# Layer 0 of a four-layer image kernel: PSUM tiles of one bank for the softmax sum and the floor, the reciprocals as side steps, the scan's total as two tiles, and a second side step on the matrix engine late in the layer

## The chip, the cores and the metric

The kernel runs on one core of a Trainium2 chip. A core has five engines with a queue each: PE (matrix multiplication; the loading of its weights is shown apart as PEld), DVE (vector), ACT (activation functions), POOL (a second vector engine) and SP, which here only starts transfers. Each engine runs its instructions in program order; semaphores make one engine wait for another. PE writes its results to PSUM, which this kernel uses as eight banks of 512 float32 values (`NB`) for each of 128 partitions; DVE and ACT read them there. All else lies in SBUF, where POOL works too, and transfers (DMA) bring data from the device's memory and back.

The metric is the device time of one execution in microseconds. Before the change it is 10293.78 us, the median of three runs (10289.03 to 10293.99).

## The reference

Input is x, four images of 128 channels and 64 x 64 pixels, in float32. Four layers follow each other. The change touches layer 0 and, in one instruction, layer 1:

```python
# layer 0, for each image; n = 4096 pixels, C = 128
x1 = conv1x1(x, v_w, v_b); x2 = conv1x1(x, q_w, q_b)
weight = conv1x1(leaky(conv1x1(x2, lw1_w, lw1_b)), lw2_w, lw2_b)
bias   = conv1x1(leaky(conv1x1(x2, bw1_w, bw1_b)), bw2_w, bw2_b)
norm = sqrt(sum(q * q, axis=0));  k = q / clip(norm, 1e-4)
logits = einsum('cn,cm->nm', k, q)
mean = logits.mean(axis=0)
sparse = relu(logits - mean * w + b);  mask = sparse != 0
attn = softmax(logits * sparse, axis=0)
attn = clip(attn * mask, 1e-08)
out = einsum('cn,nm->cm', v, attn)
y = leaky(conv3x3(out, lin_w) + lin_b) + x
```

Layer 1 is a state space scan over the 4096 pixels of each image (64 states for each of 128 channels) between a convolution and two projections, layer 2 an attention whose logits are an outer product, and layer 3 a scan over all images forward and backward, with a group normalisation behind it.

## The kernel before

**Order of the layers.** `layers01` (L1189) goes through the four images. For each it runs 128 turns of layer 0 (`turn_of`, L741), and then the scan of layer 1 (`scan_stream.tile`, L923), in whose first 16 tiles some late turns of layer 0 still run (the tail). Layer 2 of an image runs beside layers 0 and 1 of the next one: `row_weights` (L1711) in the turns of layer 0, `attend` (L1776) in the scan. Layer 3 comes at the end, after 5540 us. All instructions of these layers go through a helper that keeps them in the order of the program text, so they all have line L112 in the profile and are told apart by the names of their tiles.

**A turn.** Layer 0 treats 256 query pixels at a time, a chunk. The 4096 key pixels of a chunk are taken in 8 turns of 512, so there are 16 chunks and 128 turns; `m`, the turn's number modulo 8, is its position in the chunk. A turn works on 4 key blocks of 128 by 256 queries as one tile of 128 x 1024. Turn i issues, in this order:

| step (function, line) | engine | what it does | in the profile |
|---|---|---|---|
| image (L684) | DVE, ACT | only where a chunk has been finished (`ended`): scales it into a padded image | ypad<-acc,rows |
| weights(i) (L596) | DVE | relu(logits - cut) times logits | e<-t,lg |
| floor_of (L675) | PE | once a chunk (position 2): the floor, 1e-8 times the softmax sum, spread over the partitions | zs_rz<-rows,floor_c |
| product(i - 11) (L632) | PE | attention times values, summed over the 8 turns of a chunk | acc<-t,vT |
| logits(i + 2) (L584) | PE | keys times queries; two buffers of two banks, so those of turn i must have been read by weights(i) | lg<-rows,k |
| above(i + 1) (L591) | DVE | logits minus cut | t<-lg,rows |
| floored(i - 10) (L629) | DVE | maximum with the floor | t<-t,zs_rz |
| side steps that are not PE's, up to two | ACT, DVE, POOL | see below | |
| signs, shifted, exp | ACT, POOL, ACT | mask; subtract a bound; exponential | t<-t; e<-e,rows; e<-e |
| row weights (`beside`) | ACT | from turn 22, images 2 to 4 only | junk<-gp,... |
| masked(i - 1) (L623) | DVE or POOL | mask times exponential; on DVE in odd turns, on POOL in even ones | t<-t,e |
| sums (L608) | PE | every second turn: softmax sums Z over keys | zs_rz<-e,ones |
| one side step | PE, or another | see below | |

In a turn with `ended` the logits come before the product, because the product needs the accumulator that the image has just read.

**PSUM.** Of the eight banks, four hold the two buffers of logits (or of scan input), one ("a", `misc`) is shared by all side steps, one ("b", `other`) holds the accumulator, and two ("cd") are one tile: in layer 0 zs_rz, with Z in its first bank (`bank["zs"]`) and the reciprocals (`bank["rz"]`) and the floor (`bank["fl"]`) in the two halves of its second; in the scan `total`, over which the scan's outputs are summed. Only the last chunk's floor lies in bank "b", since "cd" is the scan's by then.

**Scale.** After a chunk's last turn its sums are turned into a scale in five steps (`scales`, L644): kept copies Z to SBUF (ACT, rows<-zs_rz, at the end of position 0), turned makes a column of it (PE, zs_rz<-quarter,rows, position 1), inverted takes the reciprocal (DVE, rzt<-zs_rz, position 2), spread brings it back over the partitions (PE, zs_rz<-ident,rzt, position 2), copied puts it into SBUF (ACT, rows<-zs_rz, position 3). They stand at fixed places in `turn_of` (`run[0][1]` to `run[0][4]`).

**Side steps.** Work that isn't bound to a turn lies in a queue of runs (`Queue`, L31), each a list of steps that is finished before the next is begun. In each turn up to two steps that are not PE's are taken after floored, and at the end either one step of PE's, if one is next, or one other. A step of PE's writes the one bank "a", and the steps behind it read it. The runs are: thresholds (L542), eight steps a chunk (two of PE's: th_ps<-rows,w_T with kbar_rep, and th_ps<-rows,lw_rep with bw_rep; then ACT's hidden and mean, DVE's times, cut, top and top_b); the 3 x 3 convolution (L696), four steps a chunk (two of PE's, then ACT and POOL, a load and a store); values in image 1; the previous scan's last outputs at the start of images 2 to 4 (`finish` and `pass_a`); and from turn 58 on the input of the next scan (`tokens_of`), one run every third turn, which has to be done by turn 120. PE never takes more than one side step in a turn.

Of the kernel before, what the change touches and what calls it, by code (L numbers as in the profile page):

```python
# [8 lines left out]
F32 = mybir.dt.float32  # L9
BF16 = mybir.dt.bfloat16  # L10
AF = mybir.ActivationFunctionType
ALU = mybir.AluOpType
# [4 lines left out]
P = 128  # L17
# [4 lines left out]
NB = 512  # L22
# [91 lines left out]
        return call  # L114


class Memory:


# [29 lines left out]
    def other(self, name, rows=P):  # L149
        return self.psb.tile([rows, NB], F32, name=name, tag="b")  # L150

    def total(self, name="total"):
        return self.pst.tile([P, self.net.T], F32, name=name, tag="cd")


class Pools:
# [14 lines left out]
    def pair(self, name):  # L171
        return self.psd.tile([P, self.T], F32, name=name, tag=name)

    def total(self, name="total"):
        return self.pst.tile([P, self.T], F32, name=name, tag=name)


class Net:
# [221 lines left out]
    def layer0(self, b, mem):  # L400
# [8 lines left out]
        S = NC * U  # L409
        LAG = U + 2  # L410
        KB = self.T // P
        Z = Block()
        Z.S, Z.LAG = S, LAG
        misc = mem.misc
# [193 lines left out]
        def sums(i):  # L608

            m = i % U  # L610
            if "zs" not in bank:
                both_banks = mem.total("zs_rz")
                bank["zs"], bank["rz"] = both_banks[:, 0:Q], both_banks[:, NB : NB + Q]
                bank["fl"] = both_banks[:, NB + Q :]
            for j in range(J):
                r = j * P // J
                pe.matmul(
                    bank["zs"][r : r + P // J, :], self.ones[:, 0 : P // J], e[i][:, j, :],
                    start=(m == 0), stop=(m == U - 1),
                )  # L620
            mem.give(e.pop(i))
# [21 lines left out]

        def scales(c):  # L644

            zt, rz = {}, {}

            def kept():
                zt[0] = zcopy[c] = row("z")
                act.copy(zt[0], bank["zs"])  # L650

            def turned():
                for i in range(Q // P):
                    pe.matmul(
                        bank["rz"][:, i : i + 1], zt[0][:, bass.ts(i, P)], self.quarter, start=True, stop=True,
                    )

            def inverted():
                rz[0] = mem.fixed("rzt", [P, Q // P])
                dve.reciprocal(rz[0], bank["rz"][:, 0 : Q // P])  # L660

            def spread():
                for i in range(Q // P):
                    pe.matmul(
                        bank["rz"][:, bass.ts(i, P)], rz[0][:, i : i + 1].to_broadcast([P, P]), self.ident,
                        start=True, stop=True,
                    )

            def copied():
                scale[c] = row("scale")  # L670
                act.copy(scale[c], bank["rz"])

            return kept, turned, inverted, spread, copied

        def floor_of(c):  # L675

            if c == NC - 1:
                bank["fl"] = bank["b"][:, Q:]
            pe.matmul(bank["fl"], self.floor_c, zcopy.pop(c), start=True, stop=True)

        def square(x):
            return x.rearrange("p (a b) -> p a b", b=IMG)
# [48 lines left out]

        due = {}
        beside = self.row_weights(b - 1, mem) if b else lambda i: None
        run = {}

        def others(left):
            while queue and not queue.on_pe() and left:
                queue.step()
                left -= 1

        def turn_of(i):  # L741
            c, m = divmod(i, U)
            w = i - LAG
            ended = i in due
            scaled = U < i <= S + 3
            if i == 4:
                begin()
            if ended:
                d = due.pop(i)
                image(d)  # L750
                if d:
                    queue.add(convolved(d - 1))
                if d == NC - 1:
                    queue.add(convolved(d))
            if i < S:
                weights(i)
            if ended:
                logits(i + 2)
            fresh = 0 <= w < S and w % U == 0
            if fresh and w < S - U:  # L760
                floor_of(w // U)
            if 0 <= w - 1 < S:
                product(w - 1)
                if (w - 1) % U == U - 1:
                    due[i + 1] = (w - 1) // U
            if fresh and w == S - U:
                floor_of(w // U)
            if not ended:
                logits(i + 2)
            above(i + 1)  # L770
            if 0 <= w < S:
                floored(w)
            if scaled and m == 2:
                run[0][2]()
            if scaled and m == 3:
                run[0][4]()
            others(2)
            if i and i <= S and (i - 1) % 2:
                signs(i - 1)
            if i < S:  # L780
                shifted(i)
            beside(i)
            if 0 < i <= S:
                masked(i - 1)
            if scaled and m == 1:
                run[0][1]()
            if scaled and m == 2:
                run[0][3]()
            if 0 < i <= S and i % 2 == 0:
                sums(i - 2)  # L790
                sums(i - 1)
            if i and i <= S and i % U == 0:
                run[0] = scales(i // U - 1)
                run[0][0]()
            if i < S and m == 0 and c + 1 < NC:
                given(c + 1)
            if m == 1 and i < S and c + 1 < NC:
                queue.first(thresholds(c + 1))
            if i == S - 1:
                mem.give(*k.values())  # L800
            if queue and queue.on_pe():
                queue.step()
            elif queue:
                others(1)
# [22 lines left out]
    def scan_stream(self, mem, blocks, side, early=lambda k, n: None):  # L827
# [65 lines left out]
        def begun(B):  # L893
            if B.first:
                B.totals[0] = mem.total()
                for j in range(W // NB):
                    s = bass.ts(j, NB)
                    pe.matmul(B.totals[0][:, s], B.diag_d, B.u[:, s], start=True, stop=False)
                if B.begun:
                    B.begun()  # L900

        def summed(i):

            k, n = items[i]
            B = blocks[k]
            for j in range(W // NB):
                s = bass.ts(j, NB)
                for m in range(i, i + Q):
                    g = of(m)[1]
                    r = (g // O) * S  # L910
                    pe.matmul(
                        B.totals[0][r : r + S, s], self.gather[:, g % O, :], p[m][:, s],
                        start=False, stop=(B.last and n == G - Q),
                    )
            for m in range(i, i + Q):
                mem.give(p.pop(m))
# [337 lines left out]
    def layer1(self, b, mem, before, after):  # L1254
# [38 lines left out]
        def prepared(w):  # L1293

            B = Block()
            B.b_rows, B.c_rows = self.bc1[w % 2, 0], self.bc1[w % 2, 1]
            B.rows = self.d1[w % 2]

            def begin():
                B.u = mem.take("u")  # L1300
                for g in groups:
                    g.u = B.u
                if w:
                    fetch(w)

            def shared():
                for g in groups:
                    g.parts = B.parts

            def done(total):  # L1310
                dve.tensor_tensor(xc[w], xc[w], total, ALU.add)
                kept["queue"].first(*finish(w))

            groups, totals = [], {}
            for i in range(SG):
                g = Block()
                g.first, g.last, g.totals, g.done = i == 0, i == SG - 1, totals, done
                g.decay, g.carry, g.diag_d = self.A1[i], carry[:, i, :], self.diagD1
                g.way, g.at = slice(None), W - 1
                g.rows = B.rows  # L1320
                g.begun = lambda: mem.give(B.u)

                def reps(g=g, i=i):
                    n = slice(i * G, (i + 1) * G)
                    if i == 0:
                        shared()
                    g.b_rep, g.c_rep = (self.rep_rows(mem.take("rep"), sp, r[n, :]) for r in (B.b_rows, B.c_rows))

                def over(g=g, i=i):
                    mem.give(g.b_rep, g.c_rep)  # L1330
                    if i == SG - 1:
                        mem.give(*B.held)

                g.reps, g.over = reps, over
                groups.append(g)
            return B, groups, begin
# [604 lines left out]
    def layer3(self):  # L1941
# [4 lines left out]
        with self.pool("l3w", 1) as big, self.pool("l3", 2) as work, self.pool("l3t", 2) as tmp, \  # L1946
# [263 lines left out]
            for forward in (True, False):  # L2210
                for ch in range(NT) if forward else reversed(range(NT)):
# [3 lines left out]
                    for j in range(J):  # L2215
# [19 lines left out]
                        B.reps = reps  # L2235

                        def done(total, K=K, j=j):
                            dve.tensor_tensor(K.sz[:, j, :], K.sz[:, j, :], total, ALU.mult)
                            if j == J - 1:
                                into(K.number + 1, post(K))  # L2240

# [131 lines left out]
```

## Time and profile before

| | us |
|---|---|
| median of 3 runs | 10293.78 |
| the profiled execution, time | 10278.34 |
| its span | 10276.6 |
| PE busy | 8433.4 (82%) |
| DVE busy | 9216.1 (90%) |
| ACT busy | 6242.1 (61%) |
| POOL busy | 8158.9 (79%) |
| layer 0 of image 1, 84 to 725: PE / DVE busy of 641 | 623.8 / 604.2 |
| layer 0 of image 2, 1615 to 2330: PE / DVE busy of 715 | 673.5 / 627.8 |
| layer 0 of image 3, 3220 to 3930: PE / DVE busy of 710 | 667.6 / 627.4 |
| layer 0 of image 4, 4815 to 5525: PE / DVE busy of 710 | 667.8 / 626.1 |
| layer 3, 5540 to 10276: PE / DVE busy of 4736 | 3637.6 / 4172.2 |

A line of the timeline has the start, the length, the engine, the source line, the operation, the tile that is written, an arrow, the tiles that are read, shapes and the number of instructions put together; in square brackets stands the idle time before it and what ended it. A line of the waits has the waiting engine and tile, the engine and tile it waited for, and then the sum in microseconds, the number of waits and the longest. A matrix product in float32 is two passes, so four products show as "x8". The profile names as releaser the event that came last.

### The profile page before, as it was taken

What the parts mean: (1) busy time and instruction counts of PE and PEld (TensorE: products, weight loads), DVE (VectorE), ACT (ScalarE), POOL (GpSimd) and SP (SyncE); (2) the same over time, 40 slices, a digit from 0 to 9 for tenths busy, and PEclk for the clock granted to TensorE, in tenths of its full rate; (3) what the DMA queues carried; (4) which work ended last, traced back from release to release, by engine and by line L of the source; (5) the groups of instructions that cost most, each with busy time, mean ns of one, the idle gap of its engine ahead of it and who ended that gap; (6) DMA issues with size and microseconds to landing.
All of it is one profiled execution on the core that took longest, in us unless ns stands there. A gap on an engine that the chain in (4) does not pass through costs nothing. (4 is left out here: it accounts for less than half of the span.)

```text
span 10276.6 us, 105974 instructions
## 1 busy us (share of the span) xinstructions
PE 8433.4 (82%) x35245; PEld 4118.2 (40%) x35320; DVE 9216.1 (90%) x6491; ACT 6242.1 (61%) x9105; POOL 8158.9 (79%) x3574
## 2 busy tenths in 40 slices
PE   8996778998888998888998877877777777777774
PEld 6772225773334774333774322322222222222221
DVE  7999999889999889999889998079999999999996
ACT  3335554666774666765565765466666666667664
POOL 5778887778887778887767887079999999999986
PEclk9998778999999999998999988989898899998886
DMA  1027882018884017885006986078788888888886
GB/s 40 17 65 193 205 198 59 18 48 200 212 209 109 18 29 182 210 209 145 24 18 146 212 201 154 16 179 208 197 205 201 203 206 205 221 223 222 225 225 176
DMA packets 523460, 1549.32 MB, mean 151 GB/s; under 512 B 85760, under 2 KB 126336, under 8 KB 522912
## 3 DMA queue, kind: packets, MB, share of 16 engines
q1 hardware_dynamic: 522912, 1542.54, 60.7%
q8 instruction: 280, 4.59, 0.2%
q14 instruction: 268, 2.20, 0.1%
HBM read 1346.52 MB, written 132.83 MB: 144 GB/s over the span
## 5 line engine op out<-in xcount | busy, mean ns | idle before, releaser
L112 DVE TENSOR_TENSOR_SCAN h<-da,carry,db 128x1024 f32<-128x1024 f32 x1536 | 3603.5, 2346 | 151.2 <-DVE db L112 2.4
L112 POOL TENSOR_TENSOR p<-h,rep 128x1024 f32<-128x1024 f32 x1024 | 2403.6, 2356 | 588.0 <-DVE h L112 523.1
L112 POOL TENSOR_TENSOR p<-h,c_rep 128x1024 f32<-128x1024 f32 x1024 | 2405.5, 2361 | 301.9 <-DVE h L112 282.9
L112 PE MATMUL db<-parts,sel 96*128 96x512 bf16 x4096 | 1366.5, 419 | 1330.1 <-DVE h L112 1322.5
L112 ACT ACTIVATE da<-row,A 128x1024 f32<-128x1024 f32 x1536 | 1760.2, 1147 | 184.6 <-DMA row<-d 182.8
L112 POOL TENSOR_TENSOR e<-e,rows 128x1024 f32<-128x1024 f32 x512 | 1261.1, 2468 | 458.2 <-DVE e L112 345.1
L112 PEld LDWEIGHTS <-sel 96*128 96x128 bf16 x4096 | 313.6, 101 | 2764.5 <-DVE h L112 1605.3
L112 DVE TENSOR_TENSOR_SCAN h<-db,carry,x 128x1024 f32<-128x1024 f32 x512 | 1195.5, 2335 | 132.0 <-ACT db L112 96.0
L112 ACT ACTIVATE db<-db,A 128x1024 f32<-128x1024 f32 x512 | 555.1, 1084 | 1034.4 <-PE db L112 985.8
L112 PE MATMUL total<-p,gather 128*32 128x512 f32 x8192 | 1171.6, 691 | 8.7 <-POOL p L112 8.7
L112 ACT ACTIVATE e<-e 128x1024 f32<-128x1024 f32 x512 | 540.6, 1056 | 933.6 <-POOL e L112 933.4
L112 PE MATMUL lg<-rows,k 128*128 128x256 f32 x4096 | 989.3, 385 | 56.1 <-DVE e L112 35.6
L112 PE MATMUL acc<-t,vT 128*128 128x256 f32 x4096 | 1002.7, 390 | 13.2 <-DVE t L112 7.6
L112 DVE TENSOR_TENSOR db<-b_rep,db 128x1024 f32<-128x1024 f32 x768 | 927.3, 1207 | 56.6 <-PE db L112 56.6
L112 PE MATMUL acc<-e,values 128*128 128x512 f32 x1536 | 852.5, 649 | 129.9 <-ACT e L112 107.2
L112 DVE TENSOR_TENSOR db<-rep,db 128x1024 f32<-128x1024 f32 x768 | 928.0, 1208 | 32.4 <-PE db L112 32.1
L112 PEld LDWEIGHTS acc<-t,vT 128*128 128x128 f32 x4096 | 783.5, 194 | 193.5 <-issue 59.5
L112 PEld LDWEIGHTS lg<-rows,k 128*128 128x128 f32 x4096 | 777.3, 192 | 204.1 <-issue 80.8
L112 ACT ACT_TABLE_LOAD x609 | 781.3, 1283 | 38.6 <-DMA r<-y 12.0
L112 DVE TENSOR_TENSOR t<-lg,rows 128x1024 f32<-128x1024 f32 x512 | 622.9, 1217 | 123.9 <-PE lg L112 123.2
L112 DVE TENSOR_TENSOR t<-t,zs_rz 128x1024 f32<-128x1024 f32 x480 | 580.5, 1209 | 134.2 <-ACT rows L112 127.4
L112 ACT ACTIVATE e<-gq,below,fcol 128x512 f32<-128x512 f32 x768 | 611.1, 805 | 141.6 <-PE acc L112 141.5
(241 smaller groups left out, 12353.0 us busy)
## 6 DMA issues: line engine op xcount, KB each, us to landing
row<-d SPq DMA_DIRECT2D x2048, 512.0 KB
rep<-bc SPq DMA_DIRECT2D x128, 512.0 KB
parts<-split SPq DMA_DIRECT2D x960, 64.0 KB
d<-delta SPq DMA_DIRECT2D x80, 384.0 KB
r<-y SPq DMA_DIRECT2D x48, 512.0 KB
res<-x SPq DMA_DIRECT2D x32, 512.0 KB
b_rep<-bc SPq DMA_DIRECT2D x32, 512.0 KB
c_rep<-bc SPq DMA_DIRECT2D x32, 512.0 KB
```

The costliest lines, as they stand in the source:

```text
L112: return self.tc.keep_in_program_order(method(*args, **kwargs))
```

## The change

`Memory.total` no longer gives one tile of two banks but a small object `Total` with two tiles of one bank, "c" and "d"; `Pools.total`, which layer 3 uses, still gives one tile, as two halves and as a whole. In layer 0 Z takes a tile in "c" and the floor one in "d". The reciprocals take a tile in the side steps' bank "a", and four of the five scale steps become a run in the queue, put in at position 1 (the thresholds, put in after it, go ahead of it); kept stays where it was. From turn 58 (`FIRST`) on, a turn whose queue is longer than 8 steps takes a further step of PE's in the middle of the turn, if one is next, and up to two more other steps near its end, before the last one. In layer 1 the sum of the scan's total into xc is two instructions of 512 columns instead of one of 1024.

```diff
+class Total:
+    def __init__(self, parts, whole=None):
+        self.parts, self.whole = parts, whole
...
-    def total(self, name="total"):
-        return self.pst.tile([P, self.net.T], F32, name=name, tag="cd")
+    def bank(self, tag, name):
+        return self.pst.tile([P, NB], F32, name=name, tag=tag)
+
+    def total(self):
+        return Total([self.bank(tag, "total") for tag in "cd"])
...
-    def total(self, name="total"):
-        return self.pst.tile([P, self.T], F32, name=name, tag=name)
+    def total(self):
+        t = self.pst.tile([P, self.T], F32, name="total", tag="total")
+        return Total([t[:, bass.ts(j, NB)] for j in range(self.T // NB)], t)
...
             if "zs" not in bank:
-                both_banks = mem.total("zs_rz")
-                bank["zs"], bank["rz"] = both_banks[:, 0:Q], both_banks[:, NB : NB + Q]
-                bank["fl"] = both_banks[:, NB + Q :]
+                bank["zs"] = mem.bank("c", "zs")[:, 0:Q]
...
             def turned():
+                held["rz"] = misc("rz_ps")
                 for i in range(Q // P):
                     pe.matmul(
-                        bank["rz"][:, i : i + 1], zt[0][:, bass.ts(i, P)], self.quarter, start=True, stop=True,
+                        held["rz"][:, i : i + 1], zcopy[c][:, bass.ts(i, P)], self.quarter, start=True, stop=True,
                     )
...
             def spread():
+                held["rz"] = misc("rz_ps")
...
             def copied():
                 scale[c] = row("scale")
-                act.copy(scale[c], bank["rz"])
-
-            return kept, turned, inverted, spread, copied
+                act.copy(scale[c], held["rz"][:, 0:Q])
+
+            return [on_pe(turned), inverted, on_pe(spread), copied]
+
+        def kept(c):
+            zcopy[c] = row("z")
+            act.copy(zcopy[c], bank["zs"])
...
             if c == NC - 1:
                 bank["fl"] = bank["b"][:, Q:]
-            pe.matmul(bank["fl"], self.floor_c, zcopy.pop(c), start=True, stop=True)
+            elif "fl" not in bank:
+                bank["fl"] = mem.bank("d", "fl")[:, 0:Q]
+            pe.matmul(bank["fl"], self.floor_c, zcopy[c], start=True, stop=True)
...
             if 0 <= w < S:
                 floored(w)
-            if scaled and m == 2:
-                run[0][2]()
-            if scaled and m == 3:
-                run[0][4]()
             others(2)
+            much = i >= FIRST and len(queue) > 8
+            if much and queue.on_pe():
+                queue.step()
...
             if 0 < i <= S:
                 masked(i - 1)
-            if scaled and m == 1:
-                run[0][1]()
-            if scaled and m == 2:
-                run[0][3]()
...
             if i and i <= S and i % U == 0:
-                run[0] = scales(i // U - 1)
-                run[0][0]()
+                kept(i // U - 1)
...
+            if m == 1 and U < i <= S + 1:
+                queue.first(scales(c - 1))
             if m == 1 and i < S and c + 1 < NC:
                 queue.first(thresholds(c + 1))
...
+            if much:
+                others(2)
             if queue and queue.on_pe():
                 queue.step()
             elif queue:
                 others(1)
...
             def done(total):
-                dve.tensor_tensor(xc[w], xc[w], total, ALU.add)
+                for c in range(C):
+                    t = xc[w][:, bass.ts(c, NB)]
+                    dve.tensor_tensor(t, t, total.parts[c], ALU.add)
                 kept["queue"].first(*finish(w))
```

## The prediction

> **What bounds the kernel now.** First the busy time in stretches of 50 us through layer 0 of the second image (columns: stretch, length, then PE, PEld, DVE, ACT, POOL busy with their instructions, clock, DMA share, GB/s).
>
> ```profile
> 1800.00:1850.00 50.00, 48.56 (x280) 38.47 (x279) 44.00 (x42) 31.48 (x46) 37.20 (x16) 1.00 0.04 11
> 2050.00:2100.00 50.00, 50.00 (x264) 37.73 (x265) 43.69 (x43) 35.45 (x55) 36.34 (x16) 1.00 0.12 35
> 2100.00:2150.00 50.00, 47.10 (x272) 36.91 (x271) 44.25 (x39) 33.50 (x48) 36.18 (x16) 1.00 0.06 17
> ```
>
> PE is busy 47 to 50 of 50 us, DVE 44. PE sets the pace here, so an edit is worth the PE idle time that it removes or makes. Next the waits, of PE between 1690 and 2260 us (nearly the whole of that image's layer 0), and of DVE in all of it.
>
> ```profile
> PE zs_rz L112 <- DVE t L112: 14.5, 15, 2.3
> PE lg L112 <- DVE e L112: 3.8, 4, 1.8
> DVE t L112 <- ACT rows L112: 41.6, 13, 3.7
> DVE t L112 <- PE lg L112: 31.8, 31, 2.1
> ```
>
> PE's largest wait is for DVE's floored, before a write into zs_rz; DVE's is for an ACT copy. The timelines show both in one place.
>
> ```profile
> 1826.10 1.89 PE L112 MATMUL lg<-rows,k 128*128 128x256 f32 x8
> 1829.43 0.60 PE L112 MATMUL zs_rz<-quarter,rows 128*128 128x1 f32 x4 [1.44 <-DVE t L112]
> 1827.77 0.35 ACT L112 COPY rows<-zs_rz 128x256 f32<-128x256 f32 x1
> 1828.15 1.22 DVE L112 TENSOR_TENSOR t<-t,zs_rz 128x1024 f32<-128x1024 f32 x1 [3.55 <-ACT rows L112]
> ```
>
> The copy kept, late behind the row weights on ACT, holds floored; floored holds PE's turned, which writes the bank that it reads. PE is idle for 1.44 us, once in a chunk of eight turns.
>
> By the Trainium skill (PSUM — Partial Sum Buffer, section "PSUM bank collisions raise a hardware error") engines collide only within a bank; different banks run side by side. Kept reads one bank and floored the other, yet floored waits 3.55 us: the tile they share orders them, not the chip. By that rule alone this wait would cost nothing today; by the row it does.
>
> Last, turn 66. Turned runs at position 1 of a chunk; the last in this image's 128 turns stands at 2257.12 (turn 121), and counting back by eight puts 1956.54 in turn 65.
>
> ```profile
> 1960.34 1.89 PE L112 MATMUL lg<-rows,k 128*128 128x256 f32 x8
> 1962.07 0.61 PE L112 MATMUL zs_rz<-ident,rzt 128*128 128x128 f32 x4
> 1962.61 1.07 PE L112 MATMUL zs_rz<-e,ones 128*32 128x256 f32 x16
> 1963.61 0.70 PE L112 MATMUL th_ps<-rows,lw_rep 64*128 64x256 f32 x2
> 1964.14 0.59 PE L112 MATMUL th_ps<-rows,bw_rep 64*128 64x256 f32 x2
> 1964.66 1.99 PE L112 MATMUL lg<-rows,k 128*128 128x256 f32 x8
> 1959.80 1.21 DVE L112 TENSOR_TENSOR t<-t,zs_rz 128x1024 f32<-128x1024 f32 x1
> 1961.01 0.41 DVE L112 TENSOR_TENSOR ypad<-acc,rows 128x256 f32<-128x256 f32 x1
> 1961.33 1.21 DVE L112 SCALAR_TENSOR_TENSOR e<-t,lg 128x1024 f32<-128x1024 f32 x1
> 1964.88 0.48 DVE L112 SCALAR_TENSOR_TENSOR rows<-th_ps,lw_b,rows 128x256 f32<-128x256 f32 x1
> 1965.40 0.48 DVE L112 SCALAR_TENSOR_TENSOR rows<-th_ps,bw_b,rows 128x256 f32<-128x256 f32 x1
> 1966.93 0.42 DVE L112 TENSOR_TENSOR rows<-rows,rows 128x256 f32<-128x256 f32 x1
> ```
>
> What to see: weights(67) ends at 1962.54, and the logits that need its buffer start at 1964.66. DVE is 2.1 us ahead, no more.
>
> **The change, part by part.**
>
> *Tiles of their own.* Turned no longer waits for floored, nor do the sums. At most 14.5 us of PE idle time goes in images 2 to 4. I take 13, since some of it only brings PE sooner to a wait for weights (3.8 us today). In image 1, whose ACT has no row weights, the same waits are five of 0.3 us: 1.5. The 4.97 us before the sums at 2293.59 go too, but there DVE runs without a gap from 2281.67 to 2306.95 and is the bound: 0, at best 5 an image. Sum: 3 x 13 + 1.5 = **40.5 us gained**, bounds 30 to 65.
>
> *Reciprocals as side steps.* Per chunk two small matmul groups (0.54 us each from start to start), a reciprocal (0.16) and a copy (0.35) move from turns 1 to 3 of a chunk to turns 4 to 6, behind the thresholds; they issue no DMA. The scale is needed ten turns after it is queued, so nothing is late. The convolution's taps slip two turns, and with them POOL's add, SP's load of the residual and store of x1. The store that the next scan's first load needs comes at turn 56, the load at 60, some 21 us later: cover enough; without it that load would be late by what is missing. At the start of images 2 to 4 the previous scan's last output steps, pass_a's matmuls and SP's stores of g2, h2 and x2 among them, end at turn 23, not 16; row weights first read at 19, after the last step that feeds them (18). All steps share the one bank "a", where today PE waits for a reader once between 1690 and 2260 (h_ps, 0.7 us). I take 0; if PE met a late copy before the taps as it now meets floored, 1.44 us a chunk.
>
> *Second PE step.* Walking the queue by the source, 17 turns per image get it: 58, 59, 66, 67, 68, 74, 75, 82, 83, 85, 90, 91, 98, 106, 107, 114, 115. What costs is that the readers follow in the same turn.
>
> (a) In 58, 66, 90, 98, 106 and 114 the second threshold matmuls run in mid turn, and times, cut and top come right after on DVE. In turn 66's rows: they start where the spread stands, 1962.07, and end 1.12 later (1963.61 to 1964.73 today), 1963.19. DVE, free at 1960.93, waits till 1963.27, and behind it wait image, weights, POOL's shifted and PE's logits. Times 0.52, cut 0.40, top 0.34, image 0.32, weights 1.21: done at 1966.06. PE ends the sums at 1964.1 (1963.13 + 1.0) and, in this turn, takes the logits before the product because an image has just ended: it waits **2.0 us**. Six times: 12.
>
> (b) In 59, 67, 91, 107 and 115 turned, reciprocal and spread fall in one turn: PE waits for drain 0.06, hand-over 0.11, reciprocal 0.16, hand-over 0.07 = 0.4, five times: 2.
>
> (c) In 74, 82 and 90 the second threshold matmuls meet ACT's hidden behind exp, row weights (1.22 each) or a softplus with two table loads (1.28 + 0.69 + 1.28). In turn 82 the logits end at 2047.72; first threshold matmuls 1.11 and sums 1.0 make PE ready at 2049.8, while the row weights hold ACT till 2050.5 and hidden (0.47) ends at 2050.97: 1.2. For the two longer ones 2.4: 6 in all, bounds 0 and 12. Image 1: 0.5.
>
> (d) In 68 DVE's reciprocal waits for ACT's root with two table loads; in 85 the taps wait for a copy behind exp: 1.25 each, bounds 0 and 3. Image 1: 1.
>
> Images 2 to 4: 12 + 2 + 6 + 2.5 = 22.5; image 1: 12 + 2 + 1.5 = 15.5. **Lost: 83 us**, bounds 30 (half of (a), little else) and 125.
>
> PE's granted clock matters too: after 3.67 us of idling the logits at 1638.22 took 3.75 us, not 1.9; after 1.82 us at 2110.17 they took 1.97. The new gaps are like the second, so the sum has nothing for it. The Trainium skill (TensorE: Matmul & The Clock Gate, section "What's actually happening") halves the clock after an idle window of about 3.4 us; by it the sum stays as it is, while the 2.86 us after a 2.76 us gap at 1657.15 speak for 0.9 more on the longest.
>
> *Total as two tiles.* 16 sums over 1024 columns (1.14 from start to start) become two of 512 (0.59, as the residual's at 1648.70): 0.04 x 16, about 1 us. Layer 3 keeps its one tile: 0.
>
> **Sum.** -40.5 + 83 + 1 = +43.5 us on the profiled 10278.3, so 10321.8. The median of the runs is 15.4 above the profiled one; on that basis 10337.
>
> **Rivals.** *A, faster.* DVE loses 41.6 us of waits an image; should that lead stay, the stalls of (a) vanish. It decides once weights ends within 1.0 us of the second threshold matmuls. Against it: in (a) DVE waits for a matmul that PE reaches after its own logits, so lead doesn't help. Cost zero: 10293.8 - 40.5 + 1 = 10254; with the tails 10234. Chance 0.20. *B, no difference:* half of the stalls hidden, 10293.8 - 40.5 + 41.5 + 1 = 10296. Chance 0.12. *C, slower still:* the gap moves instead of going, with bank "a" holding PE before the taps in each chunk; the 40.5 are not gained: 10378. For it: one bank for four kinds of steps. Against: that single 0.7 us today. Chance 0.13. *That it doesn't do what it says:* floored and sums wait as before through another tile; for the stalls that is C's time and sits in its chance. My forecast: 0.55, its own range 10316 to 10365.
>
> **Numbers.** A change within 0.2% (20.6 us) can't be told from none. Faster is A, 0.20; the same is B, 0.12; slower is the forecast and C, 0.68. The range runs from 10255, where only A's better half is left out, to 10395, C with a little of the clock's loss.
>
> **What would show it.** Right: no wait of floored for an ACT copy; no gap before the turned matmuls; six gaps of about 2 us per image before logits, each after times, cut and top with DVE waiting for th_ps; PE at 50 of 50 before turn 58; each image's first 58 turns shorter, the rest longer. Wrong: if logits follow the sums in those turns without a gap, A holds; if PE waits before conv_ps all through, C.

## The result, and the profile after

The changed kernel takes 10393.9 us (median of 4 runs, 10387.7 to 10402.6) against 10293.9 (4 runs, 10289.0 to 10297.5) for the kernel before on the same chip: ratio 1.0098, 95% interval 1.0081 to 1.0116. It is 100 us slower; 43.5 were forecast. The profiled execution took 10394.0 us (span 10392.2), that of before 10278.3 (span 10276.6). That pair is 115.6 us apart, because the one of before lay 15 us under its median.

Set side by side by the starts of DVE's weights (512 in each kernel) and of its scans (2048), in us:

| stretch, summed over the images | before | after | difference |
|---|---|---|---|
| layer 0, turn 0 to turn 56 | 1128.6 | 1117.2 | -11.4 |
| layer 0, turn 56 to the first scan tile | 1536.8 | 1638.4 | +101.6 |
| layer 1's scans of images 1 to 3 | 2768.4 | 2790.8 | +22.4 |
| first scan tile of image 4 to the last scan instruction | 4708.8 | 4711.0 | +2.2 |

The first part got shorter and the part with the second PE step longer, as the forecast has it. Busy times in stretches of 50 us of the changed kernel's second image (columns as before: stretch, length, PE, PEld, DVE, ACT, POOL, clock, DMA share, GB/s); turn 58 lies at about 1935:

```profile
1830.00:1880.00 50.00, 49.50 (x281) 38.50 (x281) 47.57 (x42) 32.24 (x48) 36.98 (x16) 1.00 0.05 12
...
2130.00:2180.00 50.00, 46.62 (x247) 36.76 (x245) 42.54 (x40) 31.78 (x45) 32.91 (x15) 0.93 0.04 12
```

Before turn 58 PE is busy for 49.5 of 50 us and the idle time that the turned matmuls had is gone. Later PE loses 3.4 us in 50, and the clock is 0.93, not 1.00. The waits of PE and DVE between 1718 and 2306 us (us in total, times, longest):

```profile
DVE t L112 <- PE lg L112: 35.1, 30, 3.5
DVE rows L112 <- PE th_ps L112: 27.2, 8, 5.9
PE lg L112 <- DVE e L112: 22.2, 14, 3.1
PE th_ps L112 <- ACT rows L112: 6.6, 4, 2.6
```

PE's 14.5 us before zs_rz and DVE's 41.6 us for the ACT copy are gone. In their place DVE waits 27.2 us for the threshold matmuls, and PE 22.2 us (3.8 before) for DVE's weights. The timeline shows one such place, turn 98 of image 2:

```profile
2167.34 1.89 PE L112 MATMUL lg<-rows,k 128*128 128x256 f32 x8
2169.20 0.70 PE L112 MATMUL th_ps<-rows,lw_rep 64*128 64x256 f32 x2
2169.74 0.59 PE L112 MATMUL th_ps<-rows,bw_rep 64*128 64x256 f32 x2
2170.19 2.37 POOL L112 TENSOR_TENSOR t<-t,e 128x1024 f32<-128x1024 f32 x1 [1.64 <-ACT t L112]
2170.26 1.07 PE L112 MATMUL zs<-e,ones 128*32 128x256 f32 x16
2170.45 0.48 DVE L112 SCALAR_TENSOR_TENSOR rows<-th_ps,lw_b,rows 128x256 f32<-128x256 f32 x1 [3.06 <-PE th_ps L112]
2170.97 0.49 DVE L112 SCALAR_TENSOR_TENSOR rows<-th_ps,bw_b,rows 128x256 f32<-128x256 f32 x1
2171.49 1.35 DVE L112 TENSOR_TENSOR rows<-rows,rows 128x256 f32<-128x256 f32 x1
2172.76 0.41 DVE L112 TENSOR_TENSOR ypad<-acc,rows 128x256 f32<-128x256 f32 x1
2173.10 1.20 DVE L112 SCALAR_TENSOR_TENSOR e<-t,lg 128x1024 f32<-128x1024 f32 x1
...
2174.45 3.58 PE L112 MATMUL lg<-rows,k 128*128 128x256 f32 x8 [3.12 <-DVE e L112]
```

DVE is 3.06 us early and waits for matmuls that PE reaches only after its logits. Times, cut, top, image and weights follow, and PE, done with the sums at 2171.3, waits 3.12 us. Two things are new: top takes 1.35 us, not the 0.42 of turn 66 before, and the logits behind the gap take 3.58 us, not 1.9, at a granted clock of 0.54. Such gaps stand before the logits after turns 58, 66, 90, 98, 106 and 114 of every image, 13.3 us together in image 1 and 16.6 to 17.0 in the others, 64 in all. After turn 24, 19 logits of the four images took over 3 us, 3.55 on average: 18 of the 24 behind these gaps, and those of turn 75 in image 2 (3.78 us), shortly behind another wait of PE, of 2.57 us for an ACT copy before the threshold matmuls.

### The profile page after: what moved, and what is told of

The parts are those of the page before. It is cut to its first block, busy times and chain, and to the rows that moved or that the text cites. A ratio compares the mean times of both kernels' runs of the same rounds, so it can differ in the third digit from the quotient of the medians.

```text
span 10392.2 us, 105806 instructions
## 1 busy us (share of the span) xinstructions
PE 8492.4 (82%) x35320; PEld 4128.5 (40%) x35320; DVE 9232.9 (89%) x6507; ACT 6240.6 (60%) x9105; POOL 8168.8 (79%) x3574
## 3 DMA queue, kind: packets, MB, share of 16 engines
q14 instruction: 268, 2.19, 0.1%
## 5 line engine op out<-in xcount | busy, mean ns | idle before, releaser
L112 PE MATMUL lg<-rows,k 128*128 128x256 f32 x4096 | 1021.5, 394 | 129.4 <-DVE e L112 107.0
L112 DVE TENSOR_TENSOR db<-rep,db 128x1024 f32<-128x1024 f32 x768 | 928.2, 1209 | 40.7 <-PE db L112 40.5
L112 POOL TENSOR_TENSOR t<-t,e 128x1024 f32<-128x1024 f32 x256 | 616.0, 2406 | 119.4 <-ACT t L112 119.4
```

Of the source, the lines that this page charges most:

```text
L112: return self.tc.keep_in_program_order(method(*args, **kwargs))
```

## The experiments

Theory M: the tiles of their own gain what was forecast, and the second threshold matmuls in mid turn, with their readers behind them, lose it again and more. Rivals: the scan total as two tiles costs the scans (S); the wait moves to another place of the chunk, bank "a" above all (C). All kernels were timed in five rounds against the kernel before on their chip.

| kernel | median us | before | ratio, 95% interval |
|---|---|---|---|
| own_banks | 10253.8 | 10297.5 | 0.9960, 0.9946 to 0.9973 |
| own_again (the same kernel) | 10266.4 | 10293.8 | 0.9972, 0.9961 to 0.9984 |
| side_early | 10270.3 | 10288.5 | 0.9983, 0.9974 to 0.9992 |
| hold_second | 10291.1 | 10297.5 | 0.9995, 0.9987 to 1.0004 |
| hold_both | 10294.1 | 10293.8 | 0.9999, 0.9990 to 1.0008 |
| six | 10295.7 | 10288.5 | 1.0009, 1.0000 to 1.0018 |
| top_later | 10342.7 | 10288.5 | 1.0051, 1.0037 to 1.0065 |
| warm4 | 10366.4 | 10288.5 | 1.0075, 1.0062 to 1.0088 |
| warm | 10372.7 | 10297.5 | 1.0073, 1.0061 to 1.0086 |
| one_tile | 10404.7 | 10297.5 | 1.0107, 1.0093 to 1.0121 |

A second measure is layer 0 alone in the profiled executions (the first two rows of the table above, added): before 2665.4, after 2755.6, own_banks 2618.1, own_again 2625.0, side_early 2628.9, six 2660.8, hold_both 2665.6, hold_second 2676.3, top_later 2708.0, warm4 2727.9, warm 2737.9, one_tile 2776.7. It leaves out the scans, whose time differs from one profiled execution to the next (see the end).

**own_banks: the tiles alone.** The kernel before, with

```diff
-                both_banks = mem.total("zs_rz")
-                bank["zs"], bank["rz"] = both_banks[:, 0:Q], both_banks[:, NB : NB + Q]
-                bank["fl"] = both_banks[:, NB + Q :]
+                both = mem.bank("c", "zs_rz")
+                bank["zs"], bank["rz"] = both[:, 0:Q], both[:, Q:]
+                bank["fl"] = mem.bank("d", "fl")[:, 0:Q]
```

and the total in two tiles, as in the change.

> The kernel before with one part of the change alone: Z and the reciprocals share one bank, the floor has a bank of its own, the scan total is two tiles; reciprocals stay at their fixed turns and no second PE step is taken. Theory M (the change's loss is made by the second PE step, its tiles gain): the waits of the reciprocal matmuls for floored go, 13 us in each of images 2 to 4 and 1.5 in image 1, so 40 us faster than before, about 10255 (10245 to 10265). Rival S (the two-tile total makes layer 1's scans some 23 us longer): 10275 to 10280, with the scans of images 1 to 3 longer as in the changed kernel. Rival C (the wait moves elsewhere in each chunk): within 10 us of the kernel before, 10284 to 10304.

> own_banks once more, beside hold_both on one chip: 40 us faster than the kernel before, ratio 0.996. What then still lies between it and hold_both is the price of the reciprocals as side steps with the few second steps left: by the prediction 0 to 10 us, by side_early (16 us raw, 24 by ratios) 16 to 24.

Measured: 10253.8, and 10266.4 in the second round of runs, 44 and 27 us under the kernel before beside them. In layer 0 the two gain 47 and 40 us. The waits of PE and DVE from 1690 to 2280 us of own_banks:

```profile
PE lg L112 <- DVE e L112: 5.6, 4, 3.0
...
PE zs_rz L112 <- ACT rows L112: 3.2, 7, 1.2
```

No wait for floored is left, and DVE no longer waits for the ACT copy. C falls for this part. This is the fastest version found, faster than both kernels.

**one_tile: the changed kernel with that part undone.**

```diff
-                bank["zs"] = mem.bank("c", "zs")[:, 0:Q]
+                both_banks = mem.total().whole
+                bank["zs"], bank["fl"] = both_banks[:, 0:Q], both_banks[:, NB + Q :]
```

with the total one tile of two banks and added in one operation.

> The changed kernel with Z, floor and the scan total back in one two-bank tile; the reciprocals stay side steps and the second PE step stays. Theory M: floored waits for the ACT copy again and DVE loses its lead, but the reciprocal matmuls no longer write that tile and only the sums can meet floored, so 0 to 15 us slower than the changed kernel, about 10400. Rival S (the two-tile total costs the scans 23 us): 10 to 25 us faster than the changed kernel, 10370 to 10384.

Measured: 10404.7, 11 above the changed kernel (their intervals overlap; in layer 0 it is 21), as M has it. S falls too: with the one-tile total the scans of images 1 to 3 take 2790.3 us, with two tiles 2790.8, and hold_second below, also with two, has 2770.4. What the two tiles do cost is read from the groups of instructions: 16 additions of 1205 ns (19.3 us) became 32 of 674 (20.8).

**hold_second: no second threshold matmuls in mid turn.**

```diff
-            if much and queue.on_pe():
+            if much and queue.on_pe() and not getattr(queue.run[0], "late", False):
```

with that mark set on the step second alone. The queue then takes other steps at other turns.

> The changed kernel, except that the second PE step never takes a chunk's second threshold matmuls, so that times, cut and top no longer run in the turn in which those matmuls were issued. Theory M: the six gaps per image before the logits go (17.0 us in images 2 to 4, 13.3 in image 1, so 64), and with them the half clock of the logits behind them (18 times 1.75, so 31); the waits of the second threshold matmuls for ACT come in three turns as now, a few us more. About 95 us faster than the changed kernel, 10298 (10285 to 10320). Rival S or a rival in which bank a or the DVE is what costs: at most 40 us faster, 10355 or above.

Measured: 10291.1, 103 us under the changed kernel. At turn 98 of image 2 the timeline has:

```profile
2143.14 1.07 PE L112 MATMUL zs<-e,ones 128*32 128x256 f32 x16
...
2144.67 0.59 PE L112 MATMUL th_ps<-rows,bw_rep 64*128 64x256 f32 x2
2145.20 1.99 PE L112 MATMUL lg<-rows,k 128*128 128x256 f32 x8
```

The threshold matmuls come after the sums, their readers a turn later, and the logits follow without a gap. M stands.

**six: that step alone, put onto own_banks.**

```diff
+            mid = i in (58, 66, 90, 98, 106, 114)
+            if mid:
+                queue.step()
...
+            if mid:
+                others(2)
```

> The kernel with banks of its own (own_banks, 10253.8) plus one thing: in turns 58, 66, 90, 98, 106 and 114 the second threshold matmuls run in mid turn and their readers in the same turn, as the changed kernel has it; reciprocals at their fixed turns, no other second step. Theory M: this alone makes six gaps of 2.2 to 3.1 us before the logits (64 over the four images) and the half clock behind most of them (31): 95 us slower than own_banks, 10349 (10335 to 10360). The prediction's term (a), 2.0 us each and no loss of clock: 48 us slower, 10302. Rival A (DVE's lead covers it): 10254 to 10270.

Measured: 10295.7, 42 us above own_banks by the medians and 50 by the ratios, 29 and 38 above own_again, and 39 over their mean in layer 0: about what the prediction's term (a) gives, and half of what I expected here or less. The rows of turn 98 in image 2 show why:

```profile
2143.00 0.71 PE L112 MATMUL zs_rz<-ident,rzt 128*128 128x128 f32 x4
...
2146.45 1.97 PE L112 MATMUL lg<-rows,k 128*128 128x256 f32 x8 [1.74 <-DVE e L112]
```

At its fixed turn the spread still gives PE some 0.6 us of work there, top takes 0.62 us, the gaps are 1.55 to 1.80 us (in turn 90 of images 2 to 4 PE waits 1.77 before the threshold matmuls instead), and none of the logits behind these gaps is slow (those after the 1.77 us wait in image 2 take 2.97). My 95 had taken over the changed kernel's gaps. The step's price isn't fixed: a gap of 1.7 us mostly costs itself, one of 2.2 to 3.1 itself and, more often than not, the clock.

**warm and warm4: the gap filled.** Spare matmuls that nothing reads, on PE at the end of the six turns, with eight and with four matmuls. They write the unused half of the floor's bank, so the rows call their tile fl:

```diff
+            if i in (58, 66, 90, 98, 106, 114):
+                for n in range(4):
+                    pe.matmul(bank["spare"], key_block(n), qs[c], start=True, stop=True)
```

> The changed kernel with eight spare matmuls (the shape of one turn's logits, about 1.9 us together, written to an unused half bank and read by nothing) put on PE at the end of turns 58, 66, 90, 98, 106 and 114, where PE now idles 2.2 to 3.1 us. They do no useful work. Theory M with the clock (after these gaps the logits run at about half the granted clock, 3.6 us and not 1.9, some 18 times): PE no longer idles long there, the logits take 1.9 us again, 25 to 31 us faster than the changed kernel, about 10365. Rival: the slower logits are not what the time is made of, or the clock falls for another reason: within 5 us of the changed kernel, or slower by what of the 1.9 us sticks out of the gap.

> The changed kernel with four spare matmuls at the end of turns 58, 66, 90, 98, 106 and 114 in place of the eight of the kernel warm, where eight took 3.72 us and outlasted the gap. They do no useful work. Four take some 1.9 us and fit into the gaps of 2.2 to 3.1. Clock theory: the logits behind take 1.9 us, not 3.6, and nothing sticks out: 31 us faster than the changed kernel, 10363 (10355 to 10370), that is 5 to 15 faster than warm. Rival: the spare work only moves the loss: within 8 us of the changed kernel.

The eight took 3.72 us, not 1.9 (a turn's logits are four such matmuls, which the rows count as eight), so they outlasted the gap; 21 us were gained all the same. Four fit:

```profile
2162.22 1.99 PE L112 MATMUL fl<-rows,k 128*128 128x256 f32 x8
...
2165.41 1.97 PE L112 MATMUL lg<-rows,k 128*128 128x256 f32 x8 [1.20 <-DVE e L112]
```

DVE's work is where it was and the logits start no earlier, yet they take 1.97 us. The granted clock over them is 1.00. The kernel gains 27 us by the medians (24 by the ratios, 28 in layer 0) by adding work. That is the price of the clock behind the six gaps: the 18 slow logits of the changed kernel took 28.2 us more than 1.97 each. It is a net figure. In turn 90 of images 3 and 4 the spare matmuls themselves took 3.35 and 3.27 us, and the logits of turn 75 are slow in images 2 to 4 here, in the changed kernel only in image 2.

**top_later: the gap shortened.**

```diff
-            elif queue:
+            elif queue and not much:
                 others(1)
```

> The changed kernel, except that a turn with a full queue doesn't take its last other step, so that top (1.35 us on DVE beside POOL's product in images 2 to 4, 0.42 in image 1) runs a turn later, and image and weights follow cut directly. Theory M: the gap before the logits shrinks from 3.1 to 1.8 us (images 2 to 4) and from 2.2 to 1.8 (image 1), some 20 us, and after gaps this short the logits keep the full clock (31): 51 us faster than the changed kernel, 10343 (10335 to 10360). Rival (the clock falls after any new gap, however short): 20 us faster, 10374.

Measured: 10342.7, 51 us under the changed kernel, as expected. At the same place the row is:

```profile
2164.21 1.97 PE L112 MATMUL lg<-rows,k 128*128 128x256 f32 x8 [1.73 <-DVE e L112]
```

In images 2 to 4 the gap at the later turns fell from 3.12 to 1.73 us, about the 1.35 of top, and the clock stayed at 1.00 over the logits behind it. In image 1 two of six logits were slow even after 1.73.

**side_early: the reciprocals alone.** own_banks, with the reciprocals of chunks 0 to 5 as side steps (turned, inverted, spread and copied as in the change), the others at their fixed turns.

> own_banks (10253.8) with the reciprocals of chunks 0 to 5 as side steps in the queue and bank of the others, those of chunks 6 to 15 at their fixed turns, no second PE step: tells what the reciprocals cost as side steps where nothing else changes. The prediction's term: 0, 10254 (10248 to 10260). Theory M after the traces (in images 2 to 4 the last scan's output steps spread over more turns and PE meets a late reader there): 10 us slower, 10264 (10259 to 10275).

Measured: 10270.3, 4 and 16 us above the two runs of own_banks (11 and 24 by the ratios); in layer 0 it is 7 us over their mean. The intervals of side_early and own_again overlap, so the cost is small and its size uncertain.

**hold_both: no threshold matmuls at all in mid turn.** As hold_second, with the mark on first as well.

> The changed kernel, except that the second PE step takes no threshold matmuls at all, neither the first nor the second pair: it is left with four turns an image (69, 77, 79, 85). Theory M: beside the gaps of hold_second (10291.1) also the waits of the second threshold matmuls for the ACT copy behind exp and the row weights go (2.46, 0.89, 1.2 and 0.43 us in image 3, 1.2 in image 1, some 15 us in all): 10276 (10268 to 10284). Rival (these waits only come back before the taps or the reciprocals' matmuls of the same bank): 10288 to 10296.

Measured: 10294.1, no faster than hold_second by the medians; layer 0 is 11 us shorter, the scans 14 longer. How much is gained stays open, but the rival's mechanism is there. The waits for an ACT copy behind exp and the row weights went from the thresholds to the next step of the same bank, as in turn 69 of image 2:

```profile
1972.23 0.71 PE L112 MATMUL rz_ps<-ident,rzt 128*128 128x128 f32 x4 [0.29 <-DVE rzt L112]
...
1974.56 0.35 ACT L112 COPY rows<-rz_ps 128x256 f32<-128x256 f32 x1
...
1974.96 3.31 PE L112 MATMUL var_ps<-mean_c,du 128*128 128x1 f32 x16 [2.02 <-ACT rows L112]
```

Two PE steps in a turn through one bank, with an ACT reader between them, cost PE 2.0 us here and 0.85 to 2.56 us in turns 74, 82 and 90 of the changed kernel, with ACT at exp and the row weights, though the steps differ.

## Why the prediction was half right

The direction and the mechanism held, the size didn't. In layer 0 the terms come to:

| term | forecast | measured | from |
|---|---|---|---|
| tiles of their own | -40.5 | -44 | mean of own_banks and own_again against before |
| reciprocals as side steps | 0 | +7 | side_early |
| (a), the gaps themselves | +48 | +64 | six gaps an image in the trace |
| clock behind the six gaps | 0 | +28 | changed kernel against warm4 |
| (b), (c), (d) | +35 | +35 | what is left of the 90 |
| layer 0 | +42.5 | +90 | 2755.6 - 2665.4 |

*Tiles of their own* is right, with its mechanism: own_banks has neither the waits of turned and the sums for floored nor DVE's wait for kept, and of bounds of 30 to 65 it takes 44.

*Reciprocals: "I take 0".* A little too low. In images 2 to 4 the changed kernel and side_early have a gap of 1.3 us before the logits at turn 21, in images 3 and 4 another at turn 13, which own_banks hasn't. The prediction saw that the last scan's output steps would end at turn 23, not 16, and priced it at nothing. With the queue later, DVE runs times, cut and top directly before weights at turn 21, and top takes 1.90 us there (side_early, image 3); own_banks has it a turn earlier, at 0.42.

*(a)* was found at the right six turns, with the right chain. 2.0 us holds for image 1 (2.19, once 2.35), not for the others: there four of six gaps were 2.8 to 3.1. I took top at 0.34 from turn 66, where it took 0.42 busy; at turns 90 to 114 of images 2 to 4 it takes 1.35. By the Trainium skill (SBUF — State Buffer, section "Who interferes with whom") a DVE operation with two inputs in SBUF contends with a GpSimd instruction that reads SBUF. The trace fits: top has two such inputs and runs beside POOL's product, which starts at 2170.19 and lasts 2.37 us. In top_later, off that place, it takes 0.61; in hold_second, beside another POOL instruction, 2.56. The contention as such wasn't tried apart from the move.

*The clock is the step that failed: "The new gaps are like the second, so the sum has nothing for it".* That set gaps of 2.0 us beside one of 1.82 that had cost nothing. They came out at 2.2 to 3.1, and 18 of the 24 logits behind them ran at about half speed (3.54 us on average for 1.97). The 2.86 us after the 2.76 us gap at 1657.15, which the prediction mentioned and didn't count, was the nearer row. The clock, put at nothing, cost 28 us; (a), put at 48, cost 64. Together they are 44 of the 48 us missed in layer 0.

*(b) to (d)* fit in sum, though the sum measured is only what the other rows leave. Of (c), the trace shows 2.56, 0.85 and 2.43 us, 5.84 an image for the 6 forecast; of (d), 1.44 for the root and 0.8 for the taps, 1.25 each forecast. That is 25 us over the images for the 27 forecast. Of (b), PE waits 0.26 us before the spread at each of the five turns named: 1.3 an image, 5.3 in all for the 8 forecast. The other 5 us of the 35 are not traced to a place.

*Total as two tiles:* 1.5 us for the 1 forecast.

*The rivals.* A fell: DVE's lead was there (3.06 us early at turn 98) and didn't help, as the prediction argues. B fell with the 100 us. C fell as it was put, for the taps, yet hold_both shows its mechanism for other steps of bank "a".

Outside layer 0 the profiled pair differs by a further 25 us, where the forecast had 1. The medians, 100 us apart, leave about 10 of it, and no part of the change was found that makes it. This stays open.

## What to carry to other kernels

Before a step is moved earlier on one engine, ask where its readers go: an in-order engine that is ahead turns its lead into a wait the moment it is given a reader of work not yet reached. Price a new gap with what follows it, the clock included, by the nearest row of its own length and not by a shorter one. Where the two halves of a change can be built apart, build them apart: here the half that gained 27 to 44 us was hidden by the other.

## What the runs showed of the hardware

**The length of a gap and the clock.** Logits directly behind an idle gap of PE, from turn 24 of each image on, in all twelve profiled kernels:

| gap, us | logits | over 3 us |
|---|---|---|
| 0.30 to 1.25 | 82 | 0 |
| 1.25 to 1.70 | 25 | 1 |
| 1.70 to 2.00 | 40 | 2 |
| 2.00 to 2.50 | 21 | 9 |
| 2.50 to 3.00 | 14 | 9 |
| 3.00 to 3.30 | 21 | 15 |

Between 1.7 and 3 us the loss goes from rare to usual. In the changed kernel the granted clock is 0.50 to 0.61 over each of the 19 logits that took over 3 us, and 1.00 over those of 1.97. Slow logits behind a gap before another step, as in turn 75, are not in the table. The Trainium skill (TensorE: Matmul & The Clock Gate, section "What's actually happening") has the clock halve after at least one idle window of about 3.4 us, counted by a window that runs freely. That equal gaps sometimes cost and sometimes don't would fit such a window, which no run here shows directly; that gaps of 2.0 to 2.5 us halved the clock in 9 of 21 cases doesn't fit a wholly idle one, and here the measurement decides.

**The scans.** Their instructions are the same in all kernels but for the total, yet the scans of images 1 to 3 took from 2768.4 us (before) to 2796.9 (six) in the profiled executions, and image 3's alone 929.1 to 944.9. In two windows the same value matmuls of image 2's scan run at another clock, first in before, then in the changed kernel:

```profile
2978.00:2982.00 4.00, 4.00 (x19) 2.54 (x18) 3.96 (x4) 1.45 (x4) 3.84 (x2) 1.00 1.04 247
2982.00:2986.00 4.00, 4.00 (x20) 2.65 (x19) 3.28 (x3) 1.95 (x5) 3.86 (x3) 0.98 0.56 137
```

```profile
3024.00:3028.00 4.00, 4.00 (x11) 2.32 (x10) 3.87 (x3) 2.43 (x4) 4.00 (x2) 0.53 0.83 225
3028.00:3032.00 4.00, 4.00 (x13) 2.65 (x13) 0.55 (x1) 0.00 (x0) 2.82 (x2) 0.50 0.01 3
```

At a clock near 0.5 PE did 11 and 13 matmuls where it did 19 and 20, with DVE idle for most of the second stretch; the scan lost 4.1 us there. Whether the stretch at half clock falls on such steps wasn't tied to any part of the change.
